# Last group of a two-layer graph network: another hand-written order of the same pieces, and four norms moved from ScalarE to VectorE

## The chip, the cores and the metric

The kernel runs on one core of a Trainium2 chip. The metric is the device time of one execution in microseconds; a lower number is better. A core has TensorE (PE, with its weight loads as PEld), VectorE (DVE), ScalarE (ACT), GpSimd (POOL) and SyncE (SP), which here only issues DMAs. Each works off its own list of instructions in order and waits on semaphores for the others.

## What is computed

128 graphs of 128 nodes with 512 features pass two attention layers, each with a residual and a layer norm. All is float32.

```python
# layer 0: 8 heads of 64
q, k, v = inputs @ Wq + bq, inputs @ Wk + bk, inputs @ Wv + bv
logits = einsum('bqhd,bkhd->bhqk', q, k) / sqrt(64)
attn = softmax(where(adj > 0, logits, -1e9))
x = layernorm(x + relu(einsum('bhqk,bkhd->bqhd', attn, v) @ Wo + bo))
# layer 1: additive attention
Wh = x @ W
e = leaky((Wh @ a1)[:, :, None] + (Wh @ a2)[:, None, :])
attention = softmax(where(adj > 0, e, -9e15), axis=1)
x = layernorm(x + leaky(einsum('bij,bjf->bif', attention, Wh)))
```

## The kernel before

The batches are worked in 32 groups of four. For a group, q, k and v come out of Strassen products (seven block products instead of eight) over all four batches; the products with Wo and with W of layer 1 are Strassen products over a pair of batches; scores, softmax and the final attention go batch by batch. A loop over the batches runs these stages as a software pipeline, several batches deep. What is still open after the loop, which is the softmaxes of the last four batches and all that hangs behind them, is worked off by a list of pieces in the string `PLAN`. The kernel is under a manual schedule: each engine gets its instructions in the order in which the code calls the pieces, so the order of the words in `PLAN` is the order of the work on all engines.

A word names a job and one of its pieces:

- `v.*` is the rest of the last v product: `p2` to `p7` are block products (four matmuls over 512 columns of output, line 366), `t2`, `t3` copies by ACT of an intermediate sum, `c11` to `c22` the output blocks (DVE, `c21` ACT), `fetch` the DMA of the next weight block. Within a Strassen product `p6` adds onto the bank of `p1` after `t0` has read it, `p7` after `t2`, `p4` after `t3`; `p3` adds onto the bank of `p5` after `c22` has read it.
- `s0` to `s3` are layer 0's attention of the last four batches: `scores` (PE), `add` (mask, DVE, line 532), `reduce` (line 541), `exp` and `divide` per head (ACT, lines 552 and 566), `store` and `fetch` (a round trip through DRAM that turns the blocks), `transpose` (DVE, line 583), `attend` (PE), `copy` (ACT, line 610), `sum` (POOL). `sl` is the batch before them.
- `a0` to `a2` are the Wo products of the last three pairs: `by` and `bw` put the bias into the banks (ACT, line 468), the Strassen pieces as above, then `stats`, `rstd`, `apply`, `store`, `fetch`, `transpose`, `sum` of layer 0's norm and the turn to features first. `al` is the pair before, whose norm is applied on DVE.
- `b0` to `b4` are the products with W of layer 1 for the last five pairs; their outputs are the `wh` tiles.
- `e0` to `e10` are layer 1's attention of the last eleven batches, `el` the one before: `sender` (ACT), `turn` (a PE transpose), `add` (ACT), `maxima` (DVE), `exp` (ACT), `divide` (DVE), `product` (PE, line 837), `copy` (ACT, line 843), `residual` (DVE, lines 847 and 848), `stats` (DVE), `rstd` (POOL), `apply`, `store`. `b3` and `b4` feed `e7` to `e10`.
- `x*`, `m*` load rows of x and the masks.

Product tiles of layers 0 and 1, scores and turns share five PSUM banks; the pairs `b1` to `b4` use the three banks of the group products. A tile takes a bank that an earlier piece in the list has freed.

A norm's `rstd` is two POOL instructions, and two more (`minus`, `shift`) if `on_scalar` is set; `apply` is then one ACTIVATE, otherwise one DVE instruction:

```python
            if self.on_scalar:
                minus = small.tile([P, 1], F32, name="minus", bufs=4)
                nc.gpsimd.tensor_scalar_mul(minus, self.mv[:, 0:1], -1.0)
                self.shift = small.tile([P, 1], F32, name="shift", bufs=4)
                nc.gpsimd.tensor_tensor(self.shift, minus, self.r, ALU.mult)

        def apply(self):
            if self.on_scalar:
                nc.scalar.activation(
                    self.src, self.src, AF.Identity, bias=self.shift, scale=self.r
                )
                return
            nc.vector.tensor_scalar(
                self.src, self.src, self.mv[:, 0:1], self.r, ALU.subtract, ALU.mult
            )
```

Of the kernel before, what the change touches and what calls it, by code (L numbers as in the profile page):

```python
# [24 lines left out]
def kernel(  # L25
# [1296 lines left out]
```

## Time and profile before

| what | us |
|---|---|
| median of three runs | 2402.37 (2400.96 to 2404.64) |
| the profiled execution | 2402.25 |
| its span | 2400.4 |
| PE, DVE, ACT, POOL busy | 2363.4, 1827.0, 1517.3, 811.1 |
| the last group's list: first matmul (`v.p5`) | 2292.41 |
| last matmuls (`e10.product`, `e9.product`) begin | 2387.25 |
| last ACTIVATE (`e9.apply`) begins | 2396.62 |

Times in the profile count from the start of the span. A line of a timeline gives the start, the duration, the engine, the line of the code and the operation, with the tiles written and read; a wait ahead of it stands in brackets with what ended it. The bars of one engine overlap[...], so a sequence is summed by the distances from start to start rather than by the durations. Names of tiles are those of the memory: `wq`, `wk` and `spare` are weights and large tiles that are no longer needed and hold other things in the last group.

### The profile page before, as it was taken

How to read it: one execution, taken by the hardware profiler on the slowest of the kernel's cores; microseconds unless marked ns; L12 is line 12 of the kernel's file. 1: busy time of each engine (PE TensorE's matmuls, PEld its weight loads, DVE VectorE, ACT ScalarE, POOL GpSimd, SP SyncE). 2: the span in 40 equal slices, each digit the busy share in tenths (PEclk: the TensorE clock that was granted, in tenths of full speed). 3: DMA queues.
4: the chain of work that ended last, by engine and by line, in shares of the span. 5: the costliest groups of instructions: out<-in, count | busy, mean ns of one | idle time of the engine just before them, and what ended most of it. 6: DMA issues, size and time to landing. Idle time of an engine off the chain costs nothing.

```text
span 2400.4 us, 44153 instructions
## 1 busy us (share of the span) xinstructions
PE 2363.4 (98%) x13362; PEld 1980.3 (82%) x13362; DVE 1827.0 (76%) x3719; ACT 1517.3 (63%) x5463; POOL 811.1 (34%) x1195
## 2 busy tenths in 40 slices
PE   8999999999999999999999999999999999999996
PEld 7888888888888888888888888888888888888874
DVE  5677787777777877877777778778778777777777
ACT  3666666566666666665666666666666666666685
POOL 1232333233333333332333433333323334333335
PEclk9999999999999999999999999999999999999999
DMA  7455555555546545555545555555554554554452
GB/s 205 158 165 160 174 163 162 176 161 158 179 147 186 164 154 174 160 165 181 159 154 183 154 176 167 156 173 157 169 181 157 157 179 155 173 175 151 156 170 98
DMA packets 435566, 395.32 MB, mean 165 GB/s; under 512 B 108280, under 2 KB 339328, under 8 KB 435328
## 3 DMA queue, kind: packets, MB, share of 16 engines
q1 hardware_dynamic: 435008, 392.23, 52.3%
q8 instruction: 107, 1.75, 0.3%
q14 instruction: 131, 1.07, 0.1%
q10 hardware_dynamic: 320, 0.26, 0.0%
HBM read 248.58 MB, written 143.72 MB: 163 GB/s over the span
## 4 chain that ended last, share of the span: by engine, by line
PE 91%; DVE 3%; DMA 2%; ACT 2%; issue 1%; SPq 1%; POOL 1%; DVEq 0%; ACTq 0%; POOLq 0%
PE st_y L366 27%; PE p_y L447 17%; PE st_w L366 13%; PE p_w L447 9%; PE st_x L366 7%; PE lg L518 6%; PE p_oT L596 5%; PE p_x L447 4%; PE p_h L837 4%; DMA wv_n<-wv 1%; ACT pa L552 0%; DMA x_dram<-x 0%; DMA wq<-in_L_gnn_Wq_dram 0%; ACT pa L566 0%; POOL rstd L648 0%
## 5 line engine op out<-in xcount | busy, mean ns | idle before, releaser
L552 ACT ACTIVATE pa<-pa,nmax 128x128 f32<-128x128 f32 x1008 | 392.6, 393 | 5.9 <-DVE nmax L541 5.5
L646 POOL TENSOR_SCALAR ve<-mv 128x1 f32<-128x1 f32 x256 | 69.9, 273 | 855.9 <-DVE mv L642 847.1
L566 ACT ACTIVATE pa<-pa,rs 128x128 f32<-128x128 f32 x1008 | 334.1, 395 | 8.6 <-DVE rs L562 8.5
L275 POOL TENSOR_TENSOR oS<-oT 128x256 f32<-128x256 f32 x63 | 45.8, 727 | 643.4 <-ACT oT L610 643.4
L532 DVE TENSOR_TENSOR pa<-lg,mf 128x512 f32<-128x512 f32 x252 | 161.9, 684 | 99.9 <-PE lg L518 99.6
L458 ACT COPY pr_t<-p_y 128x257 f32<-128x257 f32 (+1 forms) x375 | 137.7, 367 | 135.7 <-PE p_y L447 133.3
L343 ACT COPY st_t<-st_y 128x512 f32<-128x512 f32 x192 | 110.5, 575 | 144.2 <-PE st_y L366 143.1
L552 ACT ACTIVATION_READ_ACCUMULATOR pa<-pa,nmax 128x1 f32 x1008 | 192.3, 191 | 0.0
L347 ACT ACTIVATE st_t<-st_y,b_cols 128x256 f32<-128x256 f32 x192 | 80.6, 471 | 164.9 <-PE st_y L366 164.9
L648 POOL TENSOR_TENSOR rstd<-ve,mhalf 128x1 f32<-128x1 f32 x256 | 177.0, 691 | 21.4
L596 PEld LDWEIGHTS p_oT<-paT,v 128*64 128x64 f32 x2016 | 107.5, 136 | 91.8 <-PE st_y L366 44.0
L610 ACT ACTIVATE oT<-p_oT,b_cols 128x128 f32<-128x128 f32 x504 | 144.2, 368 | 60.0 <-PE p_oT L596 58.9
L583 DVE STREAM_TRANSPOSE paT<-paz 128x1024 f32<-128x1024 f32 x126 | 156.9, 1245 | 3.3 <-DMA paz<-pa_dram 2.1
L541 DVE TENSOR_REDUCE nmax<-pa 128x8 f32<-128x1024 f32 x126 | 153.7, 1220 | 4.4
L518 PE MATMUL lg<-kT,qT 64*128 64x128 f32 x2048 | 148.7, 285 | 0.0
L518 PEld LDWEIGHTS lg<-kT,qT 64*128 64x128 f32 x2048 | 124.2, 187 | 22.9 <-issue 22.9
L596 PE MATMUL p_oT<-paT,v 128*64 128x128 f32 x2016 | 137.9, 279 | 0.3 <-DVE paT L583 0.3
L768 DVE TENSOR_TENSOR wh<-p_w,pr_t 128x257 f32<-128x257 f32 x122 | 51.9, 425 | 104.0 <-PE p_w L447 64.1
L447 PE MATMUL p_y<-wo,oT 128*128 128x256 f32 x504 | 129.9, 380 | 0.7 <-ACT pr_t L458 0.6
L447 PE MATMUL p_y<-wo,oS 128*128 128x256 f32 x504 | 129.4, 379 | 0.0
L447 PE MATMUL p_y<-w,x1T 128*128 128x257 f32 x496 | 128.2, 381 | 0.2 <-DVE x1T L245 0.2
L447 PE MATMUL p_y<-w,x1S 128*128 128x257 f32 x496 | 128.0, 380 | 0.0
(201 smaller groups left out, 6032.8 us busy)
## 6 DMA issues: line engine op xcount, KB each, us to landing
pa_dram<-pa SPq DMA_DIRECT2D x126, 512.0 KB, 3.0
paz<-pa_dram SPq DMA_DIRECT2D x504, 128.0 KB, 2.8
wv_n<-wv SPq DMA_DIRECT2D x224, 256.0 KB, 2.8
x<-in_x_dram SPq DMA_DIRECT2D x128, 256.0 KB, 2.9
x_dram<-x SPq DMA_DIRECT2D x128, 256.0 KB, 2.5
xz<-x_dram SPq DMA_DIRECT2D x512, 64.0 KB, 2.0
xz<-in_x_dram SPq DMA_DIRECT2D x496, 64.0 KB, 2.2
out_dram<-z SPq DMA_DIRECT2D x120, 256.0 KB, 2.3
```

The costliest lines, as they stand in the source:

```text
L366: nc.tensor.matmul(p[:, m, :], lhs, rhs, start=start and m == 0 and kc == 0, stop=True, skip_group_check=True,)
L447: nc.tensor.matmul(p[:, :width], xs()[n][:, kc, :], w[:, PLACE[n], kc, :], start=start and kc == 0, stop=True, skip_group_check=True,)
L458: nc.scalar.copy(t[:, :width], p[:, :width])
L518: nc.tensor.matmul(self.lg[r][:, c, :], q[rows, c, cols], k[rows, c, cols], start=c == 0, stop=True, skip_group_check=True,)
L532: nc.vector.tensor_add(by_head[:, r * NC : (r + 1) * NC], self.lg[r].rearrange("p c (b k) -> p c b k", b=4), mf.unsqueeze(1).to_broadcast( ...
L541: nc.vector.tensor_reduce(self.nmax, by_head, AX.XY, ALU.max, negate=True)
L552: nc.scalar.activation(self.pa[:, :, h, :], self.pa[:, :, h, :], AF.Exp, bias=self.nmax[:, h : h + 1], accum_out=self.sums[:, h : h + 1],)
L566: nc.scalar.activation(self.pa[:, :, h, :], self.pa[:, :, h, :], AF.Copy, scale=self.rs[:, h : h + 1])
L583: nc.vector.transpose(self.paT.rearrange("p h (a i) -> p a h i", i=32), self.paz.rearrange("p a (h k) -> p a h k", k=32),)
L596: nc.tensor.matmul(self.oT[r * HD : (r + 1) * HD, c, :], v[:, h * HD : (h + 1) * HD], self.paT[:, r * NC + c, :], start=c == 0, stop=True, ...
L610: nc.scalar.activation(OT[pair][:, c, h * P : (h + 1) * P], self.oT[:, c, :], AF.Identity, bias=b_cols[:, 1, c : c + 1],)
L648: nc.gpsimd.tensor_tensor(self.r, ve, mhalf, ALU.pow)
```

## The change

The last group's list holds the same 445 pieces in another order, on all engines. Besides, `on_scalar` is false for the layer-1 norms of the last four batches (`e7` to `e10`): their `apply` is one DVE instruction instead of an ACTIVATE, and POOL makes no `minus` and `shift` for them. All before the list is as it was.

```diff
@@ -1224,57 +1224,58 @@
         jobs[f"e{n}"] = Edge(
             END - 7 + n,
             {"z": z_homes[n % 4], "e": part(wk, 6, n % 4), "att": part(wk, 5, n % 4)},
-            on_scalar=True,
+            on_scalar=n < 7,
         )
     for n in range(6):
         jobs[f"x{n}"] = jobs[f"m{n - 2}"] = Load(END - 2 + n)
     PLAN = """
-        v.p5 x0.x el.residual m1.adj s0.scores m2.adj v.fetch al.apply.0 x1.x b0.p1
-        sl.transpose al.fetch.1 v.p6 b0.t0 s0.add.0 m1.cast s0.add.1 m3.adj al.store.0
-        s1.scores s0.reduce v.t2 v.fetch v.p2 m1.mask s0.exp.4.5 s1.add.0 s1.add.1 s0.exp.6.7
-        al.fetch.0 s1.reduce b0.p6 s0.exp.0.1 b0.p5 s0.exp.2.3 v.c11 v.fetch s1.exp.4.5 v.p7
-        s0.reciprocals.1 s0.reciprocals.0 el.stats s0.divide.2.3 al.transpose.1 s0.divide.4.5
-        el.rstd b0.p2 b0.t2 al.transpose.0 s0.divide.0.1 b0.p7 al.sum.0 b0.c11 s0.divide.6.7
-        b1.p1 al.sum.1 s1.exp.6.7 s0.store al.sum.2 b0.t3 s1.reciprocals.1 s1.exp.0.1 b0.p4
-        b0.c22 al.sum.3 s1.divide.4.5 b0.p3 b0.c21 s0.fetch s1.divide.6.7 s2.scores b0.c12 v.t3
-        e0.sender e0.turn s1.exp.2.3 v.c22 v.p4 m2.cast s1.reciprocals.0 e0.add m2.mask s2.add.0
-        s1.divide.2.3 v.p3 s2.add.1 s1.divide.0.1 b1.t0 s2.reduce s1.store v.c21 b1.p6 el.apply
-        v.c12 s2.exp.2.3 el.store s3.scores e0.maxima s2.exp.6.7 s1.fetch sl.attend e0.exp
-        s2.exp.4.5 e0.divide e1.sender e1.turn b1.p5 s0.transpose sl.copy e0.product m3.cast
-        s2.reciprocals.1 sl.sum.0 e1.add m3.mask b1.p2 s3.add.0 s2.divide.6.7 sl.sum.1
-        s1.transpose s2.divide.4.5 a0.by a0.p1 sl.sum.2 b1.t2 e0.copy sl.sum.3 b1.p7 b1.c11 a0.t0
-        s3.add.1 s2.exp.0.1 a0.p6 s3.reduce b1.t3 s0.attend a0.t2 e0.residual s3.exp.0.1 a0.p7
-        s3.exp.6.7 a0.bw a0.p5 b1.c22 x2.x a0.t3 s2.reciprocals.0 e1.maxima s3.exp.2.3 a0.p4
-        s2.divide.0.1 a0.c22 b1.p3 e1.exp s3.reciprocals.0 s2.divide.2.3 a0.c21 a0.p3 e1.divide
-        s3.divide.0.1 s2.store a0.stats.1 e1.product s3.divide.2.3 b1.c12 a0.rstd.1 s3.exp.4.5
-        s1.attend e0.stats e1.copy e3.sender e3.turn s3.reciprocals.1 e0.rstd b1.p4 s0.copy e1.residual
-        s2.fetch s1.copy a0.p2 e1.stats x3.x s3.divide.6.7 a0.c11 s1.sum.0 a0.c12 s3.divide.4.5
-        s1.sum.1 e3.add s3.store a0.stats.0 s1.sum.2 e0.apply a1.by a1.p1 b1.c21 e1.rstd e0.store
-        e3.maxima a0.apply.1 e2.sender e2.turn a1.p2 a1.t0 a0.store.1 s2.transpose e3.exp a0.rstd.0 a1.p6
-        e2.add s3.fetch e1.apply e2.maxima a1.bw a1.p5 s1.sum.3 a1.t2 a0.apply.0 e3.divide a1.p7
-        e1.store e2.exp a1.c11 a0.fetch.1 s2.attend e2.divide a1.t3 a1.c22 a1.p4 s2.copy
-        a0.store.0 s3.transpose a1.p3 a1.c21 a1.stats.1 s3.attend a0.transpose.1 a0.fetch.0
-        a1.rstd.1 e3.product s3.copy a1.c12 e2.product e3.copy a1.stats.0 s3.sum.0 a2.p2
-        a1.apply.1 s3.sum.1 e3.residual e2.copy a1.store.1 a2.bw a2.p5 s3.sum.2 a0.transpose.0 a2.by a2.p1
-        a1.rstd.0 x5.x e2.residual b2.p1 a2.t0 a0.sum.0 a1.apply.0 a1.fetch.1 a2.p6 a2.c11
-        s3.sum.3 b2.t0 e2.stats b2.p5 a0.sum.1 a2.t2 e3.stats x4.x a0.sum.2 a2.p7 a1.store.0
-        a0.sum.3 b2.p6 a2.t3 e2.rstd a2.c22 a2.p4 b2.t2 a1.transpose.1 a2.p3 e3.rstd e2.apply
-        a1.fetch.0 a2.c21 b2.p7 a2.stats.1 e3.apply e4.sender e4.turn a2.c12 a2.rstd.1 b2.p2 e2.store
-        b2.t3 e3.store e4.add b2.p4 a2.stats.0 a2.apply.1 b2.c22 a2.rstd.0 b2.c21 a2.store.1
-        b2.c11 b2.p3 a1.transpose.0 e6.sender e6.turn e4.maxima a2.apply.0 a1.sum.0 b3.p1 e6.add
-        a2.store.0 a1.sum.1 b2.c12 b3.p2 e4.exp e6.maxima b3.t0 a2.fetch.1 a1.sum.2 e5.sender e5.turn
-        b3.p6 e4.divide a1.sum.3 e5.add e6.exp e5.maxima e4.product b3.t2 a2.fetch.0 e6.divide
-        e5.exp b3.p7 b3.c11 e4.copy e5.divide e6.product b3.t3 e4.residual b3.p5 e6.copy
-        e4.stats e5.product a2.transpose.0 e4.rstd b3.p4 e5.copy a2.transpose.1 b4.p2 b3.c22
-        b3.c21 a2.sum.0 e4.apply e6.residual b4.p1 a2.sum.1 e4.store b3.p3 a2.sum.2 b4.t0
-        e6.stats a2.sum.3 b4.p6 b3.c12 e6.rstd b4.c11 b4.p5 b4.t2 e5.residual b4.p7 e6.apply
-        e5.stats e8.sender e8.turn e6.store e7.sender e7.turn b4.t3 e8.add b4.p4 b4.c22 e5.rstd e7.add e8.maxima
-        b4.p3 b4.c21 e7.maxima e8.exp e10.sender e10.turn e5.apply b4.c12 e7.exp e5.store e8.divide
-        e9.sender e9.turn e10.add e7.divide e8.product e9.add e10.maxima e7.product e8.copy e9.maxima
-        e10.exp e7.copy e8.residual e9.exp e8.stats e10.divide e8.rstd e9.divide e10.product
-        e7.residual e9.product e8.apply e10.copy e8.store e7.stats e9.copy e10.residual e7.rstd
-        e10.stats e7.apply e9.residual e7.store e10.rstd e9.stats e10.apply e10.store e9.rstd
-        e9.apply e9.store
+        el.residual v.p6 x0.x m2.adj m1.adj al.apply.0 x1.x e0.sender sl.transpose s0.scores
+        al.store.0 v.t2 al.fetch.1 v.p5 el.stats m2.cast s0.add.0 m1.cast el.rstd m3.adj s0.add.1
+        s1.scores al.fetch.0 s0.reduce el.apply b0.p1 m2.mask s0.exp.4.5 el.store m1.mask
+        s2.scores s1.add.0 v.fetch s0.exp.6.7 v.fetch s1.add.1 b0.p2 s0.exp.2.3 s1.reduce
+        sl.attend s0.exp.0.1 al.transpose.0 v.p2 s1.exp.6.7 al.transpose.1 s1.exp.2.3
+        s0.reciprocals.0 al.sum.0 s0.reciprocals.1 s0.divide.0.1 v.p7 al.sum.1 v.c11 v.fetch
+        s0.divide.6.7 al.sum.2 s0.divide.2.3 al.sum.3 b1.p1 s0.divide.4.5 v.t3 s0.store b0.t0
+        v.p4 v.c22 s1.exp.0.1 b0.c11 s1.exp.4.5 s1.reciprocals.0 v.p3 s1.divide.0.1 s2.add.0
+        s0.fetch s1.divide.2.3 s2.add.1 v.c21 s2.reduce b0.p6 e1.sender m3.cast b1.p5 sl.copy
+        m3.mask v.c12 s1.reciprocals.1 s2.exp.0.1 b1.p2 sl.sum.0 s0.transpose b0.t2 sl.sum.1
+        s1.divide.4.5 b0.p7 sl.sum.2 s1.divide.6.7 sl.sum.3 s2.exp.6.7 s1.store s2.exp.2.3 b0.t3
+        s2.reciprocals.0 s2.exp.4.5 b0.p4 s2.divide.0.1 s1.fetch s2.reciprocals.1 b0.c21
+        s2.divide.6.7 s3.scores a0.by a0.bw a0.p1 s2.divide.4.5 s3.add.0 b1.t0 a0.p5 s3.add.1
+        a0.t0 e2.sender s3.reduce e1.turn b0.p5 s2.divide.2.3 s2.store a0.p6 s1.transpose
+        s3.exp.6.7 a0.p2 s3.exp.0.1 b0.c22 a0.t2 b1.p6 a0.c11 s3.exp.4.5 a0.p7 s2.fetch b1.t2
+        s3.reciprocals.1 s3.exp.2.3 b1.p7 a0.t3 s3.reciprocals.0 b0.p3 s3.divide.6.7 a0.c22
+        s3.divide.0.1 a0.p4 b0.c12 s3.divide.2.3 a0.p3 e1.add a0.c21 s3.divide.4.5 a0.stats.1
+        e2.turn b1.t3 s3.store e1.maxima e2.add a0.rstd.1 b1.p4 e2.maxima e1.exp a0.c12 e2.exp
+        a0.apply.1 e1.divide e0.turn s3.fetch s0.attend a0.stats.0 e0.add e0.maxima e1.product
+        a0.rstd.0 s0.copy s2.transpose a0.store.1 s1.attend e0.exp e2.divide e1.copy s2.attend
+        e0.divide s1.copy e1.residual e0.product a0.fetch.1 a1.by s1.sum.0 a1.p2 s2.copy
+        s3.transpose s1.sum.1 a1.p1 e0.copy x3.x s1.sum.2 b1.c11 s3.attend a0.apply.0 b1.c22
+        s1.sum.3 e0.residual e3.sender a0.store.0 b1.p3 a1.t0 a1.bw a1.p6 a1.c11 b1.c21 x2.x
+        a0.transpose.1 e4.sender e3.turn s3.copy a1.p5 b1.c12 e1.stats a0.fetch.0 a1.t2 s3.sum.0
+        e0.stats e3.add a1.p7 s3.sum.1 e3.maxima s3.sum.2 a1.t3 e3.exp a1.p4 a1.c22 s3.sum.3
+        e3.divide a1.p3 e1.rstd a1.c21 a1.stats.1 a2.by a2.bw e3.product e0.rstd a1.c12 e1.apply
+        a2.p5 e3.copy e1.store a2.p1 a1.stats.0 a1.rstd.1 e0.apply e2.product e3.residual a2.t0
+        e0.store a2.p6 a1.rstd.0 a1.apply.1 e3.stats x5.x a2.p2 e2.copy a1.store.1 a0.transpose.0
+        a2.t2 e3.rstd a1.apply.0 a2.p7 e2.residual a1.store.0 b2.p1 a0.sum.0 a2.t3 e2.stats
+        e3.apply x4.x a0.sum.1 b2.p2 a1.fetch.1 a2.c22 b2.t0 e2.rstd a2.p4 b2.c11 a2.p3 a2.c11
+        e5.sender e3.store a2.c21 a0.sum.2 e2.apply a1.fetch.0 b2.p6 a2.stats.1 a0.sum.3 e4.turn
+        a2.c12 b2.p5 a2.rstd.1 b2.t2 e4.add e2.store b2.p7 e4.maxima a2.stats.0 e4.exp e5.turn
+        b2.t3 e4.divide a2.apply.1 a2.rstd.0 b2.p4 b2.c22 a1.transpose.0 a2.store.1 b2.p3 b2.c21
+        a1.transpose.1 e6.sender b3.p1 a2.apply.0 b2.c12 a1.sum.0 e6.turn e5.add e4.product
+        a2.store.0 a1.sum.1 b3.t0 e5.maxima a2.fetch.1 e6.add a1.sum.2 b3.p5 e5.exp e6.maxima
+        e4.copy a1.sum.3 b3.p6 e5.divide e6.exp e4.residual e5.product a2.fetch.0 b3.t2 b3.p7
+        e4.stats e5.copy b3.p2 e5.residual e4.rstd b3.t3 b3.p4 b3.c11 e4.apply e6.divide
+        a2.transpose.1 e6.product b3.c21 e4.store a2.transpose.0 e8.sender e7.sender e8.turn
+        b3.c22 b4.p1 a2.sum.0 e6.copy e5.stats e8.add a2.sum.1 e7.turn b3.p3 b4.t0 e8.maxima
+        e5.rstd e6.residual e8.exp b4.p2 b4.p6 a2.sum.2 e5.apply e8.divide b3.c12 e8.product
+        a2.sum.3 b4.t2 e6.stats e5.store e7.add b4.p7 b4.c11 e8.copy e6.rstd e7.maxima e9.sender
+        b4.p5 e8.residual b4.t3 e7.exp e9.turn b4.p4 e6.apply e7.divide e6.store b4.c21 e8.stats
+        e7.product e10.sender b4.c22 e8.rstd e10.turn e7.copy b4.p3 e10.add e7.residual
+        e10.maxima b4.c12 e10.exp e8.apply e9.add e10.divide e8.store e9.maxima e10.product
+        e7.stats e9.exp e10.copy e9.divide e7.rstd e10.residual e9.product e9.copy e10.stats
+        e9.residual e10.rstd e9.stats e10.apply e9.rstd e7.apply e10.store e7.store e9.apply
+        e9.store
     """
     for piece in PLAN.split():
         name, method, *numbers = piece.split(".")
```

## The prediction

> **What bounds the kernel now.** I read the page first, then the windows of the last stage, the waits of TensorE, and the timelines of the last 110 us. The page:
>
> ```profile
> PE 2363.4 (98%) x13362; PEld 1980.3 (82%) x13362; DVE 1827.0 (76%) x3719; ACT 1517.3 (63%) x5463; POOL 811.1 (34%) x1195
> ...
> PE   8999999999999999999999999999999999999996
> ...
> DVE  5677787777777877877777778778778777777777
> ACT  3666666566666666665666666666666666666685
> ```
>
> PE is full in all slices but the first and the last. The change touches only the hand-written order of the last group, so the question is what those last two slices lose. The windows (sum of busy time; PE, PEld, DVE, ACT, POOL, then clock and DMA):
>
> ```profile
> 2306.00:2320.00 14.00, 13.84 (x95) 10.84 (x93) 9.29 (x20) 13.69 (x54) 3.79 (x6) 1.00 0.49 170
> ...
> 2334.00:2348.00 14.00, 12.08 (x70) 8.49 (x71) 11.55 (x25) 10.84 (x30) 8.22 (x18) 1.00 0.60 209
> ...
> 2376.00:2390.00 14.00, 8.36 (x24) 3.65 (x22) 10.11 (x29) 8.09 (x24) 3.65 (x11) 0.95 0.11 39
> 2390.00:2400.00 10.00, 0.00 (x0) 0.00 (x0) 4.40 (x8) 3.21 (x5) 5.02 (x12) 0.50 0.28 106
> ```
>
> ACT is full at 2306-2334, VectorE is the busiest from 2376, and TensorE is empty for the last 10 us. The waits of TensorE in 2292-2390, and where three of them lie:
>
> ```profile
> PE p_e L798 <- ACT wk L794: 4.8, 5, 2.1
> PE p_h L837 <- DVE wk L832: 3.0, 1, 3.0
> PE p_y L447 <- ACT p_y L468: 2.4, 1, 2.4
> ```
>
> ```profile
> 2335.19 1.13 PE L447 MATMUL p_y<-wo,spare 128*128 128x256 f32 x4 [2.39 <-ACT p_y L468]
> ...
> 2359.46 0.33 PE L798 MATMUL p_e<-ident,wk 128*128 128x128 f32 x1 [2.11 <-ACT wk L794]
> ...
> 2387.25 2.62 PE L837 MATMUL p_h<-wh,wk 128*128 128x512 f32 x4 [3.02 <-DVE wk L832]
> ```
>
> These are a1.p1 waiting for a1.by, e4.turn for e4.sender, and e10.product for e10.divide. The end of the timeline, on all engines:
>
> ```profile
> 2394.88 0.18 DVE L642 BATCH_NORM_AGGREGATE mv<-st 128x2 f32<-128x6 f32 x1
> ...
> 2395.14 0.22 POOL L646 TENSOR_SCALAR ve<-mv 128x1 f32<-128x1 f32 x1
> 2395.45 0.57 POOL L648 TENSOR_TENSOR rstd<-ve,mhalf 128x1 f32<-128x1 f32 x1
> 2396.09 0.23 POOL L651 TENSOR_SCALAR minus<-mv 128x1 f32<-128x1 f32 x1
> 2396.40 0.19 POOL L653 TENSOR_TENSOR shift<-minus,rstd 128x1 f32<-128x1 f32 x1
> 2396.62 0.81 ACT L657 ACTIVATE wq<-wq,shift,rstd 128x512 f32<-128x512 f32 x1 [0.74 <-POOL shift L653]
> ```
>
> DVE is done with e9's statistics at 2395.06; POOL then makes its factors and ACT applies them. After 2397.43 only the store is left: 2400.4 - 2397.43 = 2.97 us.
>
> **What the Trainium skill says.** "Perfetto Trace Analysis", Optimizing Scalar/DVE Operations: an operation that both can do may be faster on DVE, but where DVE is saturated work should rather go to Scalar. Here the apply starts the next instruction after 0.52 us on DVE and 0.71 on ACT, and DVE is the busier of the two at the end, so both halves of that advice apply. "SBUF — State Buffer", Who interferes with whom: a DVE instruction in a 2-port mode, or with two SBUF inputs, contends with a GpSimd instruction that reads SBUF. The trace agrees: the same L661 takes 0.52 alone and 0.93 beside POOL's L276/L277, and the L847 at 2346.90 takes 1.15 against 0.69.
>
> ```profile
> 2291.32 0.52 DVE L661 TENSOR_SCALAR x<-x,mv,rstd 128x512 f32<-128x512 f32 x1
> ...
> 2283.38 0.93 DVE L661 TENSOR_SCALAR z<-z,mv,rstd 128x512 f32<-128x512 f32 x1
> ...
> 2346.90 1.15 DVE L847 SCALAR_TENSOR_TENSOR wq<-wq 128x512 f32<-128x512 f32 x1
> ```
>
> **The moved applies.** Four ACTIVATEs leave ACT (4 x 0.71 = 2.8), four pairs of minus and shift leave POOL (4 x 0.59 = 2.4), four L661 come to DVE (4 x 0.52 = 2.1; up to 4 x 0.93). Only e9's is on the last chain: minus, shift and the handover there took 2396.62 - 2396.02 = 0.60, and 0.81 becomes 0.54: 0.9 us less. e10.apply and e7.apply stand in DVE's queue ahead of e9.apply, but in the 1.1 us in which POOL makes e9's rstd. e8.apply stands ahead of e10.divide, on the path: 0.52 lost there.
>
> **The order.** I sum start-to-start spacings by engine: PE 0.87 a product, 1.73 a piece of v, 1.09 scores, 1.02 attend, 0.17 turn; ACT 0.385 an exp, 0.29 a divide, 0.26 to 0.30 a small copy, 0.48 to 0.49 a 512 one, 1.03 the four of L610; DVE 0.64 an add, 1.14 the reduce, 1.17 and 0.65 the transposes, 0.72 a 512 residual step, 0.87 the stats, 0.54 maxima, 0.40 e.divide; POOL 1.54 a rstd, 0.73 a sum. The whole list is PE 79.7 in both; DVE 80.1 -> 82.2; ACT 66.9 -> 64.1; POOL 48.2 -> 45.8. So DVE's list is as long as PE's. Call lag the start of a piece less 2292.4 (the list's first matmul) less the PE work ahead of it. Before: s3.scores 0.7, a0.p1 1.1, a1.p1 4.6, e4.turn 9.3, e8.turn 11.8, e10.product 16.9 (2387.25 with 77.9 of work ahead).
>
> Then I follow the new lists by hand, each piece starting at the later of its engine and its inputs, with 0.1 to 0.2 for a handover (a copy at 2366.48 follows a matmul started at 2365.43). The first exp of s0 comes at 2298.8, as before: DVE does el.stats first, but the exps no longer stand behind v.t2. Where PE waits, in the new order:
> - v.p4: v.t3 stands behind eight exps of s0, four of s1 and eight divides: 2306.35. Lag 0.3.
> - b0.p4: b0.t3 is behind s1.divide.6.7 and four exps of s2 on a full ACT: 2298.8 + 16.7 = 2315.5, so PE starts at 2315.75. Lag 2.65: a loss that before did not have. a0.p1 waits for a0.by at 2318.15: 3.2.
> - From here ACT's list is the shorter one and DVE leads. e1.product (e1.divide behind a0.c12 and e2.maxima) 4.2; s2.attend (s2.transpose at 2333.7) 4.95; a1.p4 (a1.t3 behind e3.add and b1.c12) 6.0; a2.p3 6.65; b2.p4 (b2.t3 behind e4.exp) 7.5. At e4.turn, where before had 9.3, the lag is 6.7: a1.p1's 2.4 and e4.turn's 2.1 are gone, since by, bw and the senders now come two to five us ahead of their use.
> - e6.product (e6.divide behind the residuals of e4 and e5) 8.25; b4.p1 (a2.transpose) 8.45; e8.product 8.75; e7.product 9.15; e10.product 12.25: its maxima and divide stand behind e7.residual, b4.c12 and e8.apply. It starts at 2382.55 instead of 2387.25.
> - Tail on DVE without a gap: e9.maxima 0.54, e7.stats 0.87, e9.divide 0.40, e10 and e9 residual 1.44 and stats 0.87 each, from 2382.4: 2388.9. POOL's rstd to 2390.1, e9.apply to 2390.65, store 2.97: 2393.6.
>
> SP's queue: v.fetch for v.p7 now stands behind el.store, which waits for el.apply (2298.4); it goes out at 2299.4 and lands some 3.6 later at 2303.0, when PE wants it at 2303.6. x2.x waits for e0.residual (2340) with a0.fetch.0 behind it; that lands at 2344.4, wanted at 2350. a1.fetch.0 lands at 2359.3, wanted at 2359.5. All hidden, by 0.6, 6 and 0.2 us; if the first or third cover fails, a late landing costs PE what it is late, up to about 1 us each. The PSUM banks are those freed well earlier (s3.scores takes the banks of b0.c11 and s2.add.0).
>
> The span falls by 2400.4 - 2393.6 = 6.8. The profiled run took 2402.25, so 2395.45; the median of before is 0.12 above that run: 2395.5.
>
> **Rivals.** (1) The walk with no handovers at all ends DVE at 2388.5 and the span at 2391.5: 2393.3 us. For it: several of the waits are under 0.4. Against: every handover in the trace costs something. (2) DVE is stretched by POOL more than I put in: L661 at 0.93 four times (+1.6), and three residual pairs beside sums at 1.1 instead of 0.72 (+2.3): 2399.4 us. For it: L847 at 2346.90. Against: in the new order, too, no POOL sum is left after b4.p7, so the last 17 us are free of it. (3) Slower: the early lag on ACT (3.2 at a0.p1 against 1.1, so 2.1 more) is kept, because afterwards the longer DVE list sets the pace. DVE's stage before was 2395.06 - 2292.12 = 102.9, of which 22.8 was idle or stretched. With that same 22.8, the 82.2 list and the early 2.1, DVE ends at 2399.2, the span at 2402.2: 2404.1 us. It decides once DVE loses over 2400.4 - 2.97 - 2292.1 - 82.2 = 23.1 us; my walk has 16.3. For it: in the old order too the lag only ever grew. Against: the old losses at a1.p1, e4.turn and e8.turn have a named producer that is now early. That the order does not take effect is excluded by the instruction lists, which differ on all engines.
>
> **How the numbers follow.** My walk 0.58 (2393.5 to 2398), rival 1 0.12, rival 2 0.16, rival 3 0.14. The measurement tells 0.2% (4.8 us) from no change. Faster by over that means under 2397.6: 0.55 of the walk's case, rival 1, and 0.04 of rival 2, in all 0.71. Slower by over that means over 2407.2: rival 3 gets there where rival 2's 3.9 us come on top of it (2408.0), 0.09 of its 0.14. Within 0.2%: the rest, 0.20. The range 2391 to 2402 leaves out rival 3 and the far end of rival 1.
>
> **What would show it.** Right: PE's wait before b0.p4 of some 2 us for L458; no wait over 1 us for L468 or L794; e10.product near 2382.5; the last DVE line an L661 near 2390; ACT idle at the end. Wrong: an added wait of PE for DMA before v.p7, DVE gaps over 20 us in sum, L661 near 0.9, or e4.turn later than 2359.

## The result, and the profile after

The changed kernel takes 2399.59 us in the median of 17 runs (2395.11 to 2404.12), the kernel before beside it 2404.0 (17 runs, 2400.96 to 2406.5). The ratio is 0.9981, with an interval of 0.9974 to 0.9988: faster by 4.4 us in the medians, clear of noise, and just inside the 0.2% that the prediction takes as no change. The prediction was 2395.5, in a range of 2391 to 2402. Its gain was 6.9 us from the first median of before (2402.37); 2.5 us of that did not come, and the rest of the distance is that before itself read 1.6 us higher in this set of runs.

The profiled run of the changed kernel took 2404.12 us with a span of 2402.2. That it looks no faster than before has nothing to do with the change: its list begins (`v.p5`, or `v.p6` in the new order) at 2297.07 instead of 2292.41, though the code ahead of the list is the same. So all readings below count from the list's first matmul. From there to the end of the span ("the stage") it is 108.0 us before and 105.1 after; the walk of the prediction had 101.2. The 2.9 us between these two profiles lie at the lower edge of what the interval of the ratio allows (2.9 to 6.3 us); where the rest of the 4.4 between the medians comes from is not shown.

The busy times and the bars of the page after:

```profile
PE 2366.4 (99%) x13362; PEld 1980.3 (82%) x13362; DVE 1827.3 (76%) x3723; ACT 1515.5 (63%) x5459; POOL 808.9 (34%) x1187
...
PE   8999999999999999999999999999999999999997
...
DVE  4677787777877877877778778778777777787778
ACT  3666666666666666666666666666666666666675
```

In the bar of PE only the last slice differs, 7 instead of 6. DVE's last slice is 8 instead of 7 and ACT's last but one 7 instead of 8; other slices of these two bars differ by one here and there. Four DVE instructions more, four of ACT and eight of POOL less are the moved applies. The waits of TensorE in the last group, after (engine, tile, whom it waited for; us in total, times, longest):

```profile
PE p_h L837 <- DVE wk L832: 5.0, 5, 2.6
PE p_y L447 <- ACT wk L458: 2.7, 3, 1.8
PE st_y L366 <- DMA wv_n<-wv: 1.2, 1, 1.2
...
PE p_e L798 <- ACT wk L794: 0.8, 1, 0.8
...
PE p_y L447 <- ACT p_y L468: 0.3, 1, 0.3
```

The senders (L794) fell from 4.8 to 0.8 and the bias copies (L468) from 2.4 to 0.3, as the prediction said. In their place stand the attention weights of layer 1 (L832, from 3.0 to 5.0), the copies L458, and a weight block from DRAM that no wait of before has. The places of the four large ones, in TensorE's timeline after:

```profile
2310.59 1.97 PE L366 MATMUL st_y<-wv_n,xS 128*128 128x256 f32 x8 [1.25 <-DMA wv_n<-wv]
...
2322.35 1.14 PE L447 MATMUL p_y<-w,x1T 128*128 128x257 f32 x4 [1.83 <-ACT wk L458]
...
2390.43 1.12 PE L837 MATMUL p_h<-wh,wk 128*128 128x512 f32 x2 [2.62 <-DVE wk L832]
2392.24 1.91 PE L837 MATMUL p_h<-wh,wk 128*128 128x512 f32 x2 [0.69 <-DVE wk L832]
```

These are `v.p7`, `b0.p4`, `e10.product` and `e9.product`. With the lag of the prediction (start, less the list's start, less the PE work ahead) the stage falls into two halves of opposite sign:

| lag at | before | predicted | after |
|---|---|---|---|
| `a0.p1` | 1.1 | 3.2 | 5.06 |
| `e1.product` | 1.9 | 4.2 | 6.1 |
| `e4.turn` | 9.3 | 6.7 | 8.75 |
| `e10.product` | 16.9 | 12.25 | 15.46 |
| from `e10.product` to the end, us | 13.15 | 11.05 | 11.8 |

Up to `e1.product` the new order is 4.2 us worse; from there to `e4.turn` it loses 2.65 where the old one loses 7.4, and that turns the sign. Where that comes from shows in the windows of the two profiles, the list's start to `e1.product` and `e1.product` to `e10.product` (length, then PE, PEld, DVE, ACT, POOL busy, clock, DMA share and GB/s). Before:

```profile
2292.41:2328.74 36.33, 35.94 (x227) 29.17 (x226) 27.76 (x55) 31.10 (x124) 7.10 (x13) 1.00 0.49 156
2328.74:2387.25 58.51, 46.98 (x223) 33.04 (x221) 47.02 (x110) 37.05 (x105) 35.04 (x73) 1.00 0.40 134
```

And after:

```profile
2297.07:2337.79 40.72, 36.63 (x229) 29.34 (x228) 26.56 (x54) 33.60 (x133) 8.88 (x17) 1.00 0.52 170
2337.79:2390.43 52.64, 46.01 (x218) 32.71 (x219) 47.91 (x112) 35.03 (x94) 34.62 (x70) 1.00 0.40 126
```

In the second window VectorE has the same 47 to 48 us of work in both kernels, but is busy for 80% of it before and for 91% after. The new order packs VectorE's second half more densely, and its first half is the longer one; ACT has 2.5 us more to do there.

### The profile page after: what moved, and what is told of

It reads as the page before. It is cut to its first block, busy times and chain, and to the rows that moved or that the text cites. A ratio compares the mean times of both kernels' runs of the same rounds, so it can differ in the third digit from the quotient of the medians.

```text
span 2402.2 us, 44136 instructions
## 1 busy us (share of the span) xinstructions
PE 2366.4 (99%) x13362; PEld 1980.3 (82%) x13362; DVE 1827.3 (76%) x3723; ACT 1515.5 (63%) x5459; POOL 808.9 (34%) x1187
## 4 chain that ended last, share of the span: by engine, by line
PE 86%; DVE 4%; DMA 3%; ACT 3%; issue 1%; SPq 1%; POOL 1%; DVEq 0%; POOLq 0%; ACTq 0%
PE st_y L366 25%; PE p_y L447 16%; PE st_w L366 13%; PE p_w L447 8%; PE st_x L366 6%; PE lg L518 5%; PE p_oT L596 5%; PE p_h L837 4%; PE p_x L447 4%; ACT pa L552 1%; ACT pa L566 1%; SPq L240 1%; DMA wv_n<-wv 1%; DMA x_dram<-x 1%; DVE pa L532 1%
## 5 line engine op out<-in xcount | busy, mean ns | idle before, releaser
L275 POOL TENSOR_TENSOR oS<-oT 128x256 f32<-128x256 f32 x63 | 45.8, 727 | 639.9 <-ACT oT L610 639.9
L458 ACT COPY pr_t<-p_y 128x257 f32<-128x257 f32 (+1 forms) x375 | 137.6, 367 | 132.2 <-PE p_y L447 129.1
```

Source lines behind the costliest of these rows:

```text
L458: nc.scalar.copy(t[:, :width], p[:, :width])
```

## The experiments

Each run is set beside runs of the kernel before on its chip. "Stage" and the starts of `a0.p1`, `e1.product` and `e10.product` come from its one profiled run and count from the list's first matmul, in us. The last column gives the stretch, if there is one before 90 us, in which the granted TensorE clock of that profile was 0.50 instead of 1.00. In the cuts of `PLAN` further down, lines are shortened to the words around those that move.

| run | ratio to before | stage | `a0.p1` | `e1.product` | `e10.product` | clock 0.50 |
|---|---|---|---|---|---|---|
| before | 1 | 107.99 | 27.63 | 36.33 | 94.84 | - |
| after | 0.9981 (0.9974 to 0.9988) | 105.13 | 27.76 | 40.72 | 93.36 | - |
| order alone | 0.9984 (0.9977 to 0.9992) | 104.87 | 26.27 | 39.24 | 91.76 | - |
| applies alone | 1.0000 (0.9992 to 1.0008) | 108.87 | 27.62 | 36.32 | 96.29 | 43.2 to 46.6 |
| weights early | 0.9982 (0.9974 to 0.9989) | 105.12 | 27.62 | 40.59 | 93.25 | - |
| all early | 0.9987 (0.9979 to 0.9994) | 103.89 | 26.45 | 39.42 | 92.07 | - |
| `b0.t3` later | 0.9997 (0.9988 to 1.0006) | 106.80 | 28.21 | 41.87 | 94.46 | 26.2 to 29.7 |
| old order, producers early | 0.9995 (0.9986 to 1.0004) | 107.81 | 27.61 | 36.31 | 94.62 | 43.7 to 47.1 |
| less VectorE | 0.9970 (0.9960 to 0.9980) | 101.12 | 26.26 | 39.23 | 89.30 | - |
| less ACT | 0.9984 (0.9976 to 0.9991) | 105.04 | 27.27 | 40.23 | 92.85 | - |
| divides early | 0.9983 (0.9974 to 0.9993) | 104.47 | 26.36 | 39.71 | 92.61 | 25.5 to 28.9 |
| best | 0.9977 (0.9967 to 0.9988) | 102.20 | 24.58 | 38.41 | 90.81 | - |
| after again | 0.9986 (0.9978 to 0.9993) | 105.84 | 27.23 | 41.10 | 93.70 | 25.7 to 29.1 |

The last column matters for all that follows. It shows in windows over the same place in the list, after, "after again" and "`b0.t3` later" (columns as above, so the clock is the third from the end):

```profile
2322.77:2326.18 3.41, 3.15 (x26) 2.48 (x25) 1.72 (x4) 3.38 (x13) 0.00 (x0) 1.00 0.45 147
...
2315.56:2318.97 3.41, 3.41 (x21) 2.83 (x20) 1.75 (x3) 2.28 (x8) 0.00 (x0) 0.50 0.52 154
...
2320.44:2323.85 3.41, 3.41 (x21) 2.92 (x20) 1.31 (x3) 2.42 (x8) 0.00 (x0) 0.50 0.35 115
```

"After again" is the kernel after, unchanged. Its `b0.p4` begins 0.9 us earlier than after's, because `v.p7` waits less, and yet its `e1.product` begins 0.4 us later: the low clock costs 1.3 us there. "Applies alone" has before's list up to its last batches and is 1.2 us behind before at `a1.p7`, just past its low clock. So two profiles that differ in this column are not to be compared to better than that. In the new order the low clock follows the wait at `b0.p4`, but five other profiles have a wait of 1.7 to 1.8 us there and no low clock after it; what brings it was not tried.

### Which half of the change pays

The new order with all applies left on ACT:

```diff
-            on_scalar=n < 7,
+            on_scalar=True,
```

> The new order with all eleven norms of layer 1 still applied on ACT. If the gain is in the order (theory O), the last stage, from the list's first matmul to the end of the span, stays within 1.5 us of the changed kernel's 105.1 (before: 108.0), some 0.9 us longer for the longer chain of e9, and the ratio to before stays under 0.999. If the gain is in the moved applies (theory A), the stage goes back to about 108 and the ratio to 1.000.

The old order with the four applies on VectorE:

```diff
-            on_scalar=True,
+            on_scalar=n < 7,
```

> The old order, with only the applies of e7 to e10 on DVE. Theory O: the chain behind e9 is 0.9 us shorter, and DVE has 0.5 us more ahead of e10.divide, so the stage is 107 to 108 us and the ratio 0.9995 to 1.000. Theory A: the stage is near 105 and the ratio near 0.998.

As far as the ratios can tell, the order alone has the whole gain (0.9984) and the applies alone have none (1.0000). Between `e10.product` and the end the order alone takes 13.1 us, the profiles with the moved applies 11.8 to 12.3 ("best" apart). In "order alone" the clock is at 0.50 from `e10.product` on; beside the three with that same low clock ("after again", "less ACT" and "`b0.t3` later", 12.1 to 12.3) the moved applies are worth 0.8 to 1.0 us of the tail, near the 0.9 of the prediction. That is too little for the ratios. The stage of the applies alone says nothing on them, because of the 1.2 us that the low clock cost ahead of every piece that this edit touches. Its tail is 0.6 shorter than before's (12.6 against 13.15), but before has the low clock from 96.0 us on and this run only from 101.3.

### Where the early lag comes from

SyncE's timeline after shows the queue that the prediction followed only in part:

```profile
2299.38 0.78 SPq L712 DMA_DIRECT2D x_dram<-x  x1
...
2304.01 2.06 SPq L240 DMA_DIRECT2D xz<-x_dram  x4
2306.16 0.38 SPq L861 DMA_DIRECT2D out_dram<-z  x1
2306.64 3.06 SPq L407 DMA_DIRECT2D wv_n<-wv  x3
```

`al.store.0` goes out at 2299.38 and takes 4.6 us to land; `al.fetch.0` waits for it, then spends 2.06 us issuing its four parts; `el.store` and the weights of `v.p7` stand behind it. Those land at 2310.45 and TensorE was ready at 2309.34. The same landing holds VectorE, in its timeline after: the transposes of `al` wait for it, and the reciprocals that ACT's eight divides of `s0`, and behind them `v.t3`, need stand after them.

```profile
2307.77 1.31 DVE L245 STREAM_TRANSPOSE wq<-xz 128x512 f32<-128x512 f32 x2 [1.78 <-DMA xz<-x_dram]
2309.00 0.20 DVE L562 RECIPROCAL rs<-sums 128x4 f32<-128x4 f32 x2
```

First, only the weights were moved ahead in that queue:

```diff
-        s1.scores al.fetch.0 s0.reduce el.apply b0.p1 m2.mask s0.exp.4.5 el.store m1.mask
-        s2.scores s1.add.0 v.fetch s0.exp.6.7 v.fetch s1.add.1 b0.p2 s0.exp.2.3 s1.reduce
+        s1.scores v.fetch v.fetch al.fetch.0 s0.reduce el.apply b0.p1 m2.mask s0.exp.4.5 el.store
+        m1.mask s2.scores s1.add.0 s0.exp.6.7 s1.add.1 b0.p2 s0.exp.2.3 s1.reduce
```

> The changed kernel with two of v's weight loads ahead of al.fetch.0 and el.store in SP's queue. The wait of 1.25 us before v.p7 goes. If early lag is carried to the end (theory L), the stage shortens by 0.6 to 1.3 us, unless the softmax on ACT, which is late for a reason of its own, takes the wait over at b0.p4. If DVE's long list sets the end (theory D), e10.product starts no earlier, counted from the list's first matmul (93.4 us now), and the stage stays at 105.1 within 0.5.

`v.p7` no longer waits, and `a0.p1` gains 0.14 us. A wait stands two products further on, at `v.p4`, as TensorE's and VectorE's timelines of this run show:

```profile
2308.20 1.99 PE L366 MATMUL st_y<-wv_n,xT 128*128 128x256 f32 x8 [1.15 <-ACT st_t L343]
...
2303.82 1.30 DVE L245 STREAM_TRANSPOSE wq<-xz 128x512 f32<-128x512 f32 x2 [2.78 <-DMA xz<-x_dram]
```

This wait is largely of the edit's own making. The first part of `al.fetch.0` goes out 6.3 us after the list's first matmul, as in "order alone" (6.4), but with the weights under way it takes 4.7 us to land instead of 2.2. So the transposes of `al` begin at 11.64, against 10.70 after and 10.21 in "order alone", where neither `v.p7` nor `v.p4` waits. The reciprocals, the divides and `v.t3` stand behind them.

Then the other two chains were shortened as well: reciprocals ahead of the transposes, and `b0.t3` ahead of four exps.

```diff
-        sl.attend s0.exp.0.1 al.transpose.0 v.p2 s1.exp.6.7 al.transpose.1 s1.exp.2.3
-        s0.reciprocals.0 al.sum.0 s0.reciprocals.1 s0.divide.0.1 v.p7
+        sl.attend s0.exp.0.1 s0.reciprocals.0 s0.reciprocals.1 al.transpose.0 v.p2 s1.exp.6.7
+        al.transpose.1 s1.exp.2.3 al.sum.0 s0.divide.0.1 v.p7
...
-        s1.divide.4.5 b0.p7 sl.sum.2 s1.divide.6.7 sl.sum.3 s2.exp.6.7 s1.store s2.exp.2.3 b0.t3
+        s1.divide.4.5 b0.p7 sl.sum.2 s1.divide.6.7 sl.sum.3 b0.t3 s2.exp.6.7 s1.store s2.exp.2.3
```

> As the run with the early loads, and besides the reciprocals of s0 ahead of al.transpose on DVE (ACT waited 1.1 us for them) and b0.t3 ahead of four exps of s2 on ACT (PE waited 1.8 us for it). The lag at a0.p1 falls from 5.1 to some 2 to 3. Theory L: the stage shortens by as much, 2 to 3 us, to 102 to 103. Theory D: the lag at a0.p1 falls, but the one at e10.product stays at 15 to 15.5, and the stage at 105 within 0.7.

Now `a0.p1` is 1.3 us earlier than after, not more, because it waits 1.8 us for `a0.by`, which is still behind the exps on ACT. And `e1.product` and `e10.product` are both earlier by the same 1.3. That is what "order alone" has by chance (26.27, 39.24 and 91.76), and the ratio, 0.9987, doesn't show it. The stage of 103.9 lies between what theory L (102 to 103) and theory D (105 within 0.7) had.

The other way round, `b0.t3` and `b0.p4` were put behind two more exps and two divides:

```diff
-        s2.exp.6.7 s1.store s2.exp.2.3 b0.t3
-        s2.reciprocals.0 s2.exp.4.5 b0.p4 s2.divide.0.1 s1.fetch s2.reciprocals.1 b0.c21
+        s2.exp.6.7 s1.store s2.exp.2.3
+        s2.reciprocals.0 s2.exp.4.5 s2.divide.0.1 s1.fetch s2.reciprocals.1 b0.t3 b0.p4 b0.c21
```

> The changed kernel with b0.t3 put back behind two more exps and two divides of s2 on ACT, 1.35 us later. Theory L: the lag at a0.p1 grows only as far as a0.by, behind the same ACT list, does not already hold it, so 0 to 0.9 us, and the stage grows by just that. Theory D: b0.p4 starts 1.3 us later and the stage stays at 105.1 within 0.5.

`b0.p4` waits 3.17 instead of 1.83. But `v.p7` does not wait in this run, so `b0.p4` begins at 25.1, no later than after (25.3); that `e1.product` and `e10.product` are 1.1 us later than after comes with the low clock. The fair comparison is "order alone", where `v.p7` doesn't wait either: `b0.p4` is 1.35 later than there, `e1.product` 2.6 and `e10.product` 2.7. So about half is the longer wait and half the low clock, and all of it is still there at the end. What is lost ahead of `e1.product`, by a wait for ACT or by the clock, is lost at `e10.product`. The ratio, 0.9997, points the same way, but its interval overlaps with that of "after again".

Chance gave the same test. "Order alone", "less VectorE", "divides early", "less ACT" and "after again" have the same list as after up to `a0.p1`. In them `al.store.0` landed in 4.1, 4.1, 4.2, 4.3 and 4.4 us, against 4.6 after; `v.p7` waited 0, 0, 0, 0.75 and 0.35, against 1.25; and `a0.p1` began at 26.27, 26.26, 26.36, 27.27 and 27.23, against 27.76 (0.4 of it in "after again" is the low clock). The store is not all: the weights themselves took 3.81 us to land after, 3.40 in "less ACT" and 2.81 in "after again". So the prediction's 3.2 for the lag at `a0.p1` was nearly right for a run whose weights come in time (26.27 - 22.70 of work ahead is 3.57).

### Whether the early producers made the gain

The prediction argued that the old order's losses had named producers, and that the new order has them early. Here the old order gets just that: `a1.by`, `e4.sender`, `e8.sender` and `e7.sender` moved ahead of what held them on ACT.

```diff
-        s2.fetch s1.copy a0.p2 e1.stats x3.x s3.divide.6.7
+        s2.fetch s1.copy a0.p2 e1.stats x3.x a1.by s3.divide.6.7
...
-        s1.sum.1 e3.add s3.store a0.stats.0 s1.sum.2 e0.apply a1.by a1.p1
+        s1.sum.1 e3.add s3.store a0.stats.0 s1.sum.2 e0.apply a1.p1
...
-        e3.rstd e2.apply a1.fetch.0 a2.c21 b2.p7 a2.stats.1 e3.apply e4.sender e4.turn
+        e3.rstd e4.sender e2.apply a1.fetch.0 a2.c21 b2.p7 a2.stats.1 e3.apply e4.turn
...
-        e5.residual b4.p7 e6.apply e5.stats e8.sender e8.turn e6.store e7.sender e7.turn
+        e5.residual b4.p7 e8.sender e7.sender e6.apply e5.stats e8.turn e6.store e7.turn
```

> The old order with only four pieces moved forward on ACT: a1.by ahead of two divides of s3, e4.sender ahead of e2.apply and e3.apply, e8.sender and e7.sender ahead of e6.apply. Each of these applies waits for POOL, and PE waited for the moved pieces: 2.4, 2.1 and some 1.4 us. If the gain of the new order is that these producers are early (theory P), the stage falls from 108.0 to 103 to 105.5 and the ratio to before is 0.998 or less. If DVE's list sets the pace and the waits were only where its lateness showed (theory D), PE waits elsewhere for DVE instead and the stage stays within 1 us of 108.

In the profile `e10.product` is only 0.2 us earlier than before. TensorE's timeline of this run:

```profile
2335.04 1.13 PE L447 MATMUL p_y<-wo,spare 128*128 128x256 f32 x4 [0.27 <-ACT p_y L468]
2338.45 0.47 PE L798 MATMUL p_e<-ident,wk 128*128 128x128 f32 x1 [2.28 <-ACT wk L794]
...
2362.72 1.14 PE L447 MATMUL p_y<-w,x1T 128*128 128x257 f32 x4 [1.09 <-ACT wk L458]
```

`a1.p1` waits 0.27 instead of 2.39, and the turn behind it 2.28 instead of 0.17: 2.55 together against 2.56 before. `e4.turn` no longer waits, and a piece behind it, `b2.p4`, does.

But this profile has the low clock and before's hasn't. Windows over this place before, in "applies alone" and in this run:

```profile
2336.10:2339.52 3.42, 3.25 (x16) 2.51 (x15) 2.38 (x6) 3.20 (x10) 2.89 (x8) 1.00 0.80 273
...
2336.46:2339.88 3.42, 3.42 (x11) 2.54 (x10) 2.57 (x7) 2.79 (x8) 2.83 (x9) 0.50 0.81 289
...
2338.08:2341.50 3.42, 3.05 (x8) 2.52 (x9) 2.45 (x6) 2.22 (x8) 2.84 (x8) 0.50 0.84 285
```

"Applies alone" has the old order and a low clock of the same length at nearly the same place. Beside it `e4.turn` is 2.4 us earlier here, and `e10.product` 1.7. The medians give 1.4 us (2403.60 against 2405.03 before), in an interval that includes no change. So of some 5.5 us of waits that were taken away at `a1.p1`, `e4.turn` and `e8.turn`, 1.4 to 1.7 came out at the end, which the ratio can't tell from nothing, and the rest was waited for at the pieces behind them. Those waits are for ACT again, not for VectorE as theory D had it, and the 0.998 of theory P was not reached.

### Who sets the pace in the second half of the new order

Between `e1.product` and `e10.product` after and all its variants but one take 52.4 to 52.9 us, however late they begin. Three edits take something out of that stretch. The leaky step (L847) of `e2` to `e6` is left out, five VectorE instructions:

```diff
-            nc.vector.scalar_tensor_tensor(z, z, ALPHA, z, op0=ALU.mult, op1=ALU.max)
+            if not B - 9 <= self.b <= B - 5:
+                nc.vector.scalar_tensor_tensor(z, z, ALPHA, z, op0=ALU.mult, op1=ALU.max)
```

> The changed kernel with the leaky step of e2 to e6 left out: five DVE instructions of 0.72 us less, 3.6 us, all behind e1.product. In the new order the distance from e1.product to e10.product was 52.4 to 52.7 us in seven profiles. If DVE's list is what sets that distance (theory D2: dense in its second half), it falls by 2.5 to 3.6 us, and the stage with it. If the chain over PE and ACT sets it (theory C), it falls by under 1 us.

The applies of `a1` and `a2`, four ACTIVATEs, are left out:

```diff
-            self.norms[h].apply()
+            if self.pair < B // 2 - 2:
+                self.norms[h].apply()
```

> The changed kernel with the four applies of a1 and a2 on ACT left out: 2.8 us less on ACT in the same stretch, and 0.8 us off each round trip to x1T. Theory D2: the distance from e1.product to e10.product stays at 52.6 within 0.4. Theory C: it falls by 1 to 2.8 us.

And two divides, for which TensorE waits at L837, are drawn forward on VectorE, at the same work:

```diff
-        b1.p4 e2.maxima e1.exp a0.c12 e2.exp
-        a0.apply.1 e1.divide e0.turn
+        b1.p4 e2.maxima e1.exp e1.divide a0.c12 e2.exp
+        a0.apply.1 e0.turn
...
-        b3.p2 e5.residual e4.rstd b3.t3 b3.p4 b3.c11 e4.apply e6.divide
+        b3.p2 e6.divide e5.residual e4.rstd b3.t3 b3.p4 b3.c11 e4.apply
```

> The changed kernel with e1.divide ahead of a0.c12 and e6.divide ahead of e5.residual on DVE, so that two of TensorE's waits for a divide (0.8 and 0.6 us) go. Theory D2: DVE's list is no shorter, so the distance from e1.product to e10.product does not shrink by what e1.product gains, and the stage stays at 105 to 106 within 0.5. Theory C: the stage shortens by 0.8 to 1.4 us.

The window from `e1.product` to `e10.product` with less VectorE work (columns as in the windows above, so VectorE's busy time is the third of the five):

```profile
2328.21:2378.28 50.07, 45.54 (x218) 32.91 (x218) 44.69 (x107) 34.93 (x94) 32.44 (x70) 1.00 0.42 132
```

And with less ACT work:

```profile
2335.49:2388.11 52.62, 46.08 (x219) 32.55 (x219) 48.02 (x112) 32.34 (x90) 34.59 (x70) 0.99 0.39 126
```

VectorE's busy time falls by 3.2 us and the stretch by 2.6. POOL's, the fifth, falls by 2.2 in the same run, though it has no instruction less; POOL alone was not tried, so a part by way of POOL is not excluded. ACT's falls by 2.7 and the stretch stays. The divides took the waits of TensorE for L832 from 5.0 to 3.3 us, but those for L831 and L794 rose from 1.2 to 2.7 in sum; the stretch is 52.9. So, as far as these three edits tell, VectorE's list sets the pace of the new order from `e1.product` on, and neither ACT nor the order of the divides does. What in the old order's list held VectorE at 80% was not isolated.

### All early moves in one version

This version, "best", has the early pieces of "all early", `a0.by` and `a0.bw` ahead of the exps as well, `e10.maxima` ahead of `e7.residual` on VectorE, and only the last apply on VectorE, since only that one is on the last chain. The lines of "all early" are left out here.

```diff
-        s2.reciprocals.0 s2.exp.4.5 b0.p4 s2.divide.0.1 s1.fetch s2.reciprocals.1 b0.c21
-        s2.divide.6.7 s3.scores a0.by a0.bw a0.p1
+        a0.by a0.bw s2.exp.2.3 s2.reciprocals.0 s2.exp.4.5 b0.p4 s2.divide.0.1 s1.fetch
+        s2.reciprocals.1 b0.c21 s2.divide.6.7 s3.scores a0.p1
...
-        e7.copy b4.p3 e10.add e7.residual e10.maxima b4.c12
+        e7.copy b4.p3 e10.add e10.maxima e7.residual b4.c12
...
-            on_scalar=n < 7,
+            on_scalar=n != 9,
```

> The changed kernel with all early moves (weight loads, reciprocals, b0.t3), a0.by and a0.bw ahead of two exps of s2, e10.maxima ahead of e7.residual, and only e9's apply on DVE. Theory L (early lag is carried to the end): the lag at a0.p1 falls by another 1 to 1.8 us against the run with the early moves, and the stage from 103.9 to 101 to 102.5. Theory D: the stage falls by no more than e8.apply's 0.5 and the gaps of 0.7 us on DVE at the end, to 102.7 or more, whatever the lag at a0.p1.

The kernel after ran beside it, unchanged:

> The changed kernel as it is, once more, to see how far the stage of one profiled execution and its lags repeat. If the stage repeats within 0.5 us of 105.1, differences of 1 us between profiles can be read; if the wait for v's weights before v.p7 comes and goes, the stage comes and goes with it (theory L) or not (theory D).

The stage of "after again" repeats within 0.7 us, not the 0.5 that was asked for, with less wait at `v.p7` and the low clock against it. The early part of "best", in TensorE's timeline, is `b0.p4` and, two lines on, `a0.p1`:

```profile
2315.13 1.14 PE L447 MATMUL p_y<-w,x1T 128*128 128x257 f32 x4 [0.47 <-ACT wk L458]
2316.19 1.16 PE L518 MATMUL lg<-kT,qT 64*128 64x128 f32 x16
2317.28 1.13 PE L447 MATMUL p_y<-wo,oT 128*128 128x256 f32 x4
```

`a0.p1` is 3.2 us earlier than after, `e10.product` 2.6, the stage 2.9 (102.2, in the 101 to 102.5 of theory L). The medians on the same chip are 2398.04 and 2401.06, 2405.03 for before. The two intervals overlap, and the runs of "best" had the higher granted clock on average (0.9967 against 0.9958). Its five runs at 0.996 have a mean of 2399.8 us against 2400.6 for ten of after, its three at 0.997 have 2398.7 against 2398.9 for five. So most of the 3.0 us between the medians goes with the clock. Whether the kernel's shorter waits raise that clock or chance did is open, and that it is faster than after is not shown.

## Why the prediction was right, and where its steps failed

The sign and the range held; the gain was put 2.5 us too high. The prediction gave 0.71 to a gain of over 0.2% and 0.20 to a change within it, and the 0.19% that was measured is of the second kind. The profiled stage is 3.9 us longer than the walk: 1.9 by `e1.product`, 1.3 from there to `e10.product`, 0.7 in the tail.

- **SyncE's queue, "All hidden, by 0.6, 6 and 0.2 us".** This step failed at the first of the three. The walk let `v.fetch` go out at 2299.4, behind `el.store` and its `el.apply`. It is 2304.06 on the clock of the run after; it went out at 2306.64. The queue ahead of `el.store` holds `al.fetch.0`, which waits for `al.store.0`; the walk did not price that wait. In the old order the list's first weights go out at 2294.44, ahead of both fetches of `al`. The price was bounded nearly rightly at "up to about 1 us": 0 to 1.25 in six profiles with this list. The other two covers held; TensorE has no other wait for a DMA.
- **"b0.p4: b0.t3 is behind ... on a full ACT", lag 2.65.** Right: the wait for L458 was predicted at some 2 us and measured 1.83. The lag at `a0.p1`, 3.2, measured 5.06, of which 1.25 is `v.p7`'s.
- **"From here ACT's list is the shorter one and DVE leads".** Right, and supported by leaving work out on each. The mis-sized term is VectorE's own: 0.72 for each residual step. Three of them ran at 0.91 to 1.24 us, 1.2 more in sum than at 0.69, which is as large as the 1.3 that the stretch is longer than the walk. That the two are the same was not tried. Two of the three, in VectorE's timeline after:

```profile
2341.70 1.10 DVE L848 TENSOR_TENSOR wq<-wq,x 128x512 f32<-128x512 f32 x1
...
2379.68 1.24 DVE L848 TENSOR_TENSOR wq<-wq,x 128x512 f32<-128x512 f32 x1
```

The Trainium skill says that a VectorE instruction with two inputs in SBUF contends with a GpSimd instruction that reads SBUF ("SBUF — State Buffer", Who interferes with whom). This trace agrees: both have two inputs in SBUF and run beside a POOL sum (POOL's L275 begins at 2341.51, L277 at 2379.65).

- **"a1.p1's 2.4 and e4.turn's 2.1 are gone, since by, bw and the senders now come two to five us ahead of their use".** The waits are gone, and the loss between `e1.product` and `e4.turn` is what the walk said (2.65 against 2.5). But the reason given is at most a part of it: early producers brought the old order 1.4 to 1.7 us at the end, and the waits went to the pieces behind. What else makes the loss fall from 7.4 to 2.65 is open. The same sentence was the argument against rival 3.
- **Rival 3, "the early lag on ACT ... is kept, because afterwards the longer DVE list sets the pace".** Its mechanism is what the runs show: the lag at `e1.product` comes out at `e10.product` one for one. Its size was wrong: it gave VectorE the old order's 22.8 us of idle or stretched time. By the same sum (the end of the last apply, 2399.06, less the first residual, 2296.77, less 82.2) the new order has 20.1, between the walk's 16.3 and the 23.1 from which the rival decides.
- **Rival 2** put L661 at 0.93 beside POOL. It took 0.52 to 0.55 at the end; only its part on residual steps happened. **Rival 1**, no handovers at all, did not.
- **The tail, 11.05 us.** It took 11.8. From `e10.product` to the end of e9's statistics it is 6.74 (2397.17 - 2390.43) instead of 6.35, POOL's factor takes 0.1 more, and the store 0.2: it ends 3.14 after the last apply, not 2.97.
- **The signs.** Those for `b0.p4`, for L468 and L794 and for an idle ACT came. `e10.product` and the last L661 are 3 to 4 us later than named, counted from the list's first matmul, and one sign of being wrong came too, the wait for a DMA before `v.p7`.

The end, in the timeline after, is of the form that was predicted, with ACT idle:

```profile
2397.09 0.97 DVE L661 TENSOR_SCALAR wq<-wq,mv,rstd 128x512 f32<-128x512 f32 x2
2397.26 0.41 POOL L646 TENSOR_SCALAR ve<-mv 128x1 f32<-128x1 f32 x1 [1.33 <-DVE mv L642]
...
2397.76 0.72 POOL L648 TENSOR_TENSOR rstd<-ve,mhalf 128x1 f32<-128x1 f32 x1
2398.51 0.55 DVE L661 TENSOR_SCALAR wq<-wq,mv,rstd 128x512 f32<-128x512 f32 x1 [0.45 <-POOL rstd L648]
```

The two applies of e10 and e7 lie in POOL's time for e9's factor, as the walk had them; the last one then still waits 0.45.

## What to carry to other kernels

A wait that the profile names may only be where an engine met the pace of the others; before counting it as a gain, ask who will be met next, and test it by moving that producer alone. Where several in-order engines share a last stage, find the one whose list is nearest to full in each part of it: here, what was lost ahead of the part in which VectorE is nearly full was still lost at its end. Before two single profiles are compared to a microsecond, look at the granted clock over the same stretch of both. And when a DMA issue is moved, read the whole queue in front of it, including the store that its neighbour waits for.

## What the hardware showed that was not expected

- The 256 KB store `al.store.0` takes 2.6 us to land in the median of all such stores, but 3.5 before and 3.9 to 4.6 in the new order. The DMA engines are busy for 0.69 of that time before and for 0.89 after. Its landing, and that of the weights behind it (2.81 to 3.81 us), decide whether TensorE waits at `v.p7`.
- The list began between 2288.98 and 2297.07 us in the profiled runs of the changed list and its variants, with the same code ahead of it. That spread of 8 us is larger than the whole gain, which is why the stage and not the span of one profile was compared. The clock also falls to 0.50 far ahead of the list, in the first 110 us of most profiles; the four without that begin their list at 2288.98 to 2292.70. Whether it makes the spread was not tried.
- The granted clock fell to 0.50 for 3.4 us in the list of five of the thirteen profiles. It cost 1.2 to 1.3 us in the two kernels where a profile without it stands beside.
- The times of whole runs follow the mean granted clock. Of the runs of the kernel before beside "best", nine at 0.995 have a mean of 2407.3 us, 25 at 0.996 have 2405.0, ten at 0.997 have 2403.2 and three at 0.998 have 2402.5.
